# Dividing a block's weighted columns between ScalarE and VectorE in a graph network

## The chip, the cores and the metric

The kernel runs on one core of one Trainium2 chip. The core has TensorE (PE; its weight loads are listed as PEld), VectorE (DVE), ScalarE (ACT), GpSimd (POOL) and SyncE (SP), which run their own instruction streams in order and wait for one another by semaphores. The metric is the device time of one execution in microseconds. Three executions before the change took 3933.62, 3918.14 and 3926.89 us; the median is 3926.89 us.

## The reference

The input is a node table `x` of 6250 rows by 256 features, and 100,000 edges `src`, `dst`, sorted by `dst`. Two attention layers of one kind (four heads of 64 features, every node also an edge to itself), a residual with layer norm, then a third attention layer of another kind (eight heads of 32) and again a residual with layer norm. Cut to what matters:

```python
def _gatv2_layer(x, src, dst, n, Wl, Wr, att, b):          # H, C = 4, 64
    xl = (x @ Wl).reshape(n, H, C)
    xr = (x @ Wr).reshape(n, H, C)
    e = leaky_relu(xl[src] + xr[dst], 0.2)
    logits = einsum('ehc,hc->eh', e, att)
    alpha = exp(logits - segment_max(logits, dst)[dst]) / segment_sum(...)[dst]
    return segment_sum(xl[src] * alpha[:, :, None], dst).reshape(n, H * C) + b
...
h = _gatv2_layer(x, src, dst, n, Wl1, Wr1, att1, b1)        # layer one
h = elu(h)
h = _gatv2_layer(h, src, dst, n, Wl2, Wr2, att2, b2)        # layer two
x = _layernorm(x + h)
x = _layernorm(x + _L1_gnn_ref(x, W, a, src, dst))          # layer three
```

The change touches the product `xl[src] * alpha` of layers one and two.

## The kernel before

A first part (up to some 225 us of the profiled execution) builds tables of features in memory and orders the nodes by how many edges end in them. The nodes then form 49 blocks of 128, one node to a partition. In a block, each node's neighbours stand side by side as columns: a block with at most `c` edges to a node has `S = c + 1` columns, the first being the node itself. `S` is 39 in the first block, 26 in the second, 21 to 18 around the fifteenth, and 10 in the last; the 49 blocks have 863 columns, of which 814 are gathered. A column is 128 partitions by 4 heads by 64 features of fp32 (with one or two more numbers). The columns of a block are cut into chunks of at most nine (`chunks`), each in a buffer of its own; a pool of seven such buffers (`rowp`, `bufs=7`) lets gathers run ahead.

`layer2` runs layer one (i = 0) and layer two (i = 1) with the same loop over blocks `b`. Each engine takes its instructions in the order in which the loop writes them:

1. `start(b + 3)`, `gather(b + 1)`: POOL issues an indirect DMA for each column of the next block (L1311). In layer one `start` is one more indirect DMA on POOL (L1397), in layer two two loads on SP (L1439, L1440).
2. `ready(b + 1)`: the next block's own rows. In layer one PE transposes them (L1180), ScalarE copies the transpose (`xT`, L1182), PE multiplies (L1187); in layer two ScalarE copies a loaded row (L1446).
3. `attend(b)`: for each chunk VectorE takes the larger of gathered rows and own row (L1331), multiplies by the attention vector (L1332) and sums per head into the logits `lg` (L1333). Then `weights`: VectorE takes the largest logit (`top`, L1198), ScalarE makes four exponentials, one a head, into `wt` in PSUM with their sums `den` (L1205), and copies the weights of the last `few` columns to `by` in SBUF (L1212).
4. `end(b - 1)`: VectorE divides the sum of the block before, `acc`, by its `den` (`h`, L1348) and works on it further; ScalarE applies what is left (L1411 to L1414 in layer one, L1280 to L1288 in layer two).
5. VectorE takes the reciprocal of `den` (L1377).
6. `weighted_sum(b)`: the columns are multiplied by their weights in place. ScalarE takes the last `few` columns of the last chunk with one multiply for each column and head, 128 partitions by 64 features (L1234); VectorE takes all others with one multiply for each chunk (L1235). PE then adds up the columns in order by matmuls with an identity into `acc` in PSUM (L1242, two matmul records to a column, the second of which gives a signal).
7. The rest of block `b - 1`: PE transposes `h` or the normed row (L1180), ScalarE copies it (L1182), PE multiplies (L1187), ScalarE copies the result to a row (L1426 or L1461), SP stores it.

So a column that ScalarE weights is added on PE only after its four multiplies are signalled, and these columns are the last of the block. `few` is zero in the last block. The third layer has eight heads, passes no `few`, and adds up on VectorE.

Of the kernel before, what the change touches and what calls it, by code (L numbers as in the profile page):

```python
# [1120 lines left out]
def tile_by_degree(  # L1121
# [7 lines left out]
    NB = -(-N // P)  # L1129
# [12 lines left out]
    def per_head(t, H):  # L1142
        return t.rearrange("p (h d) -> p h d", h=H)
# [30 lines left out]
    def source(of, b, j):  # L1174
        return bass.IndirectOffsetOnAxis(ap=of[:, b, j : j + 1], axis=0)
# [13 lines left out]
    def chunks(n):  # L1189
        k = -(-n // T)  # L1190
        cut = [n * i // k for i in range(k + 1)]
        return list(zip(cut, cut[1:]))

    def weights(work, ps, lg, S, H, scalar=0):


        top = work.tile([P, H], F32, name="top")
        nc.vector.tensor_reduce(  # L1198
            top, lg[:, :S, :].rearrange("p s h -> p h s"), axis=AX.X, op=OP.max, negate=True
        )  # L1200
        wt = ps.tile([P, S, H], F32, name="wt")
        den = work.tile([P, H], F32, name="den")
        if H <= 4:
            for h in range(H):
                nc.scalar.activation(  # L1205
                    wt[:, :, h], lg[:, :S, h], AF.Exp, bias=top[:, h : h + 1],
                    accum_out=den[:, h : h + 1],
                )
            by = None
            if scalar:  # L1210
                by = work.tile([P, scalar, H], F32, name="by")
                nc.scalar.copy(by, wt[:, S - scalar :, :])  # L1212
            return (wt, by), lambda: den
        nc.vector.tensor_add(lg[:, :S, :], lg[:, :S, :], top[:, None, :].to_broadcast([P, S, H]))  # L1214
        nc.scalar.activation(wt, lg[:, :S, :], AF.Exp)  # L1215

        def add_up():
            nc.vector.reduce_sum(den, wt.rearrange("p s h -> p h s"), axis=AX.X)
            return den

        return (wt, None), add_up

    def weighted_sum(ps, rows, cut, wts, H, width, between):

        wt, by = wts
        acc = ps.tile([P, F], F32, name="acc")
        S = cut[-1][1]
        for g, (s0, s1) in zip(rows, cut):
            n = s1 - s0
            g4 = g[:, :n, : H * width].rearrange("p t (h d) -> p t h d", h=H)[:, :, :, : F // H]  # L1230
            m = n - by.shape[1] if by is not None and s1 == S else n
            for t in range(m, n):
                for h in range(H):
                    nc.scalar.mul(g4[:, t, h, :], g4[:, t, h, :], by[:, t - m, h : h + 1])  # L1234
            nc.vector.tensor_mul(  # L1235
                g4[:, :m], g4[:, :m],
                wt[:, s0 : s0 + m, :].unsqueeze(3).to_broadcast([P, m, H, F // H]),
            )
            if s0 == 0:
                between()  # L1240
            for t in range(n):
                nc.tensor.matmul(acc, ident, g4[:, t], start=s0 + t == 0, stop=s0 + t == S - 1)  # L1242
        return acc
# [46 lines left out]
    def layer2(i, table, of, width, start, own, finish):  # L1290
# [4 lines left out]
        with ExitStack() as es:  # L1295
            rowp = es.enter_context(tc.tile_pool(name=f"rows{i}", bufs=7))
            zp = es.enter_context(tc.tile_pool(name=f"z{i}", bufs=3))
            work = es.enter_context(tc.tile_pool(name=f"work{i}", bufs=3))
            ps = es.enter_context(tc.tile_pool(name=f"ps{i}", bufs=2, space=PSUM))
            ps1 = es.enter_context(tc.tile_pool(name=f"ps1{i}", bufs=1, space=PSUM))  # L1300
            pst = es.enter_context(tc.tile_pool(name=f"pst{i}", bufs=2, space=PSUM))
            at = ps1.tile([P, W2], F32, name="at")
            nc.scalar.copy(at, att[i])
            state = {}

            def gather(b):
                cut = chunks(cols[b] + 1)
                rows = [rowp.tile([P, T, width], F32, name="g") for _ in cut]
                for g, (s0, s1) in zip(rows, cut):
                    for s in range(max(s0, 1), s1):  # L1310
                        nc.gpsimd.indirect_dma_start(  # L1311
                            out=g[:, s - s0, :], out_offset=None, in_=table,
                            in_offset=source(of, b, s - 1),
                        )
                state[b] = [rows, cut]

            later = []

            def ready(b):
                pr, put = own(work, ps, pst, b, state[b][0][0][:, 0, :W2])  # L1320
                state[b].append(pr)
                later.append(put)

            def attend(b):
                rows, cut, xr = state.pop(b)
                S = cols[b] + 1
                lg = work.tile([P, CM + 1, H2], F32, name="lg")
                for g, (s0, s1) in zip(rows, cut):
                    n = s1 - s0
                    z = zp.tile([P, T, W2], F32, name="z")[:, :n, :]  # L1330
                    nc.vector.tensor_max(z, g[:, :n, :W2], xr[:, None, :].to_broadcast([P, n, W2]))  # L1331
                    nc.vector.tensor_mul(z, z, at[:, None, :].to_broadcast([P, n, W2]))  # L1332
                    nc.vector.reduce_sum(  # L1333
                        lg[:, s0:s1, :], z.rearrange("p t (h d) -> p t h d", h=H2), axis=AX.X
                    )
                few = min(S // 3, cut[-1][1] - cut[-1][0] - 1) if b + 1 < NB else 0
                wt, new = weights(work, ps, lg, S, H2, few)
                while later:
                    later.pop()()
                if i == 0:  # L1340
                    for g, (s0, s1) in zip(rows, cut):
                        s = max(s0, 1)
                        nc.scalar.copy(spots[:, b, s - 1 : s1 - 1], g[:, s - s0 : s1 - s0, W2])
                return rows, cut, wt, new

            def end(b, acc, den):
                h = work.tile([P, F], F32, name="h")
                nc.vector.tensor_mul(  # L1348
                    per_head(h, H2), per_head(acc, H2),
                    den.unsqueeze(2).to_broadcast([P, H2, D2]),  # L1350
                )
                if i == 0:
                    nc.vector.tensor_add(h, h, bias[0])
                return finish(work, pst, b, h)

            for b in range(3):
                start(work, b)
            gather(0)
            ready(0)
            later.pop()()  # L1360
            if i == 0:
                none(state[0][2])
            acc, den, rest = None, None, None
            for b in range(NB):
                if b + 3 < NB:
                    start(work, b + 3)
                if b + 1 < NB:
                    gather(b + 1)
                if b + 1 < NB:
                    ready(b + 1)  # L1370
                rows, cut, wt, new = attend(b)
                if b:
                    rest = end(b - 1, acc, den)
                if i == 0:
                    nc.vector.tensor_add(x1[:, b, :], x1[:, b, :], bias[1])
                den = new()
                nc.vector.reciprocal(den, den)  # L1377

                last = []

                def between():
                    if b:
                        last.append(rest())

                acc = weighted_sum(ps1, rows, cut, wt, H2, D2 + 1, between)
                if i == 0 and b + 1 < NB:
                    none(state[b + 1][2])
                if last:
                    last[0]()
            end(NB - 1, acc, den)()()  # L1390

    def none(t):

        nc.vector.memset(t.rearrange("p (h d) -> p h d", h=H2)[:, :, D2:], -BIG)
# [79 lines left out]
    with ExitStack() as es:  # L1474
# [59 lines left out]
        for b in range(NB):  # L1534
# [4 lines left out]
            rows, cut, wt, new = attend(b)  # L1539
# [41 lines left out]
```

## Time and profile before

| what | us |
|---|---|
| median of three executions | 3926.89 |
| the profiled execution | 3945.85 |
| its span, from the first to the last instruction | 3944.1 |
| first part and tables, up to | about 225 |
| layer one, from the first reciprocal at 225.3 to that of its last block at | 1452.4 |
| layer two, likewise, from 1534.5 to | 2689.5 |
| layer three and the end, up to | 3944.1 |
| VectorE busy over the span | 2724.0 (69%) |
| GpSimd busy | 2582.6 (65%) |
| TensorE matmuls busy | 1485.0 (38%) |
| ScalarE busy | 1102.9 (28%) |

Busy times are those of one profiled execution, which was 19 us over the median. GpSimd's busy time here is nearly all the issue of gathers. "issue" as the reason of an idle time means that the profile shows no instruction that ended it, "remote" that a signal ended it whose sender the profile doesn't tell. A group's line gives after the bar its busy time, the mean duration of one instruction in ns, and the idle time of the engine just before the group's instructions. In a timeline the columns are the start, the time taken, engine, line, operation, what is written and read, and the number of instructions merged; in brackets the idle time before and what ended it. A wait is recorded at the engine that waits; a signal's way from one engine to another is not.

### The profile page before, as it was taken

The page shows a single profiled execution, that of the slowest core. Times are in us where ns is not written, and L with a number is a line of the kernel's source. Part 1 is how long each engine was busy: PE and PEld are TensorE (multiplying, and loading weights), DVE is VectorE, ACT ScalarE, POOL GpSimd, SP SyncE. Part 2 cuts the span into 40 slices and gives each one's busy share as a digit, 9 for nine tenths or more (in the row PEclk, how much of TensorE's full clock was granted, in tenths as well). Part 3 has the DMA queues.
Part 4 walks back from the last instruction along what each step waited for, and adds up shares of the span by engine and source line. Part 5 has one row for each costly group of instructions (what it writes and reads, how often), then busy time and mean ns, then how long its engine had stood idle before and what let it go on. Part 6 is the DMA issues. An engine that isn't in the chain of part 4 may idle for free.

```text
span 3944.1 us, 23710 instructions
## 1 busy us (share of the span) xinstructions
PE 1485.0 (38%) x5144; PEld 1107.1 (28%) x5145; DVE 2724.0 (69%) x2731; ACT 1102.9 (28%) x4179; POOL 2582.6 (65%) x2640
## 2 busy tenths in 40 slices
PE   5336556556676761455545455552000000000000
PEld 4224434344554541343433343442000000000000
DVE  6277778678788876888877888983655545444554
ACT  2124334334444441343434343541000000000000
POOL 6466666666666636666666666654777777776675
PEclk7667778777788886777666767776555555555555
DMA  8443333333343424343333343433333333333332
GB/s 185 103 96 99 98 100 105 100 98 102 104 107 103 106 74 101 98 111 107 106 107 107 106 112 104 118 104 58 102 100 97 102 99 100 99 97 84 82 99 72
DMA packets 197564, 399.63 MB, mean 101 GB/s; under 512 B 63516, under 2 KB 115994, under 8 KB 197396
## 3 DMA queue, kind: packets, MB, share of 16 engines
q0 software_dynamic: 123488, 342.06, 33.6%
q1 hardware_dynamic: 66226, 54.22, 4.8%
q10 hardware_dynamic: 7698, 1.74, 0.4%
q8 instruction: 45, 0.74, 0.1%
q14 instruction: 107, 0.88, 0.1%
HBM read 357.84 MB, written 40.42 MB: 101 GB/s over the span
## 4 chain that ended last, share of the span: by engine, by line
issue 23%; POOL 22%; DVE 15%; PE 13%; another core or an unknown queue 9%; ACT 6%; DMA 2%; DVEq 0%; ACTq 0%; POOLq 0%
POOL g L1485 15%; PE acc L1242 9%; POOL g L1311 5%; DVE z L1332 4%; DVE z L1331 4%; PE pm L1187 3%; ACT g L1234 3%; DVE lg L1333 2%; ACT wt L1205 2%; DVE g L1235 1%; DVE g L1253 1%; POOL out L1525 1%; ACT xT L1182 1%; DMA g<-whs_d,spots 1%
## 5 line engine op out<-in xcount | busy, mean ns | idle before, releaser
L1242 PE MATMUL acc<-g,ident 128*128 128x256 f32 x3452 | 1038.7, 462 | 940.8 <-issue 368.9
L1242 PEld LDWEIGHTS acc<-g,ident 128*128 128x128 f32 x3452 | 778.1, 233 | 1197.6 <-issue 618.4
L1311 POOL DMA_INDIRECT g<-xl_d,spots x814 | 772.5, 949 | 465.2 <-issue 227.5
L1311 POOL DMA_INDIRECT g<-xl_d,near_r x814 | 774.8, 952 | 427.8 <-issue 239.2
L1485 POOL DMA_INDIRECT g<-whs_d,spots x814 | 857.3, 1053 | 299.0 <-issue 292.6
L1234 ACT ACTIVATE g<-g,by 128x64 f32<-128x64 f32 x2064 | 560.2, 337 | 431.4 <-issue 429.4
L1331 DVE TENSOR_TENSOR z<-g,pr 128x1820 f32<-128x1820 f32 (+4 forms) x236 | 502.3, 2129 | 60.9 <-DMA g<-xl_d,spots 31.9
L1332 DVE TENSOR_TENSOR z<-z,at 128x1820 f32<-128x1820 f32 (+4 forms) x236 | 503.8, 2135 | 8.1
L1333 DVE TENSOR_REDUCE lg<-z 128x28 f32<-128x1820 f32 (+4 forms) x236 | 503.6, 2134 | 8.2
L1235 DVE TENSOR_TENSOR g<-g,wt 128x1792 f32<-128x1792 f32 (+5 forms) x236 | 354.0, 1518 | 2.9
L1215 ACT ACTIVATE wt<-lg 128x128 f32<-128x128 f32 (+17 forms) x49 | 14.0, 285 | 849.3 <-DVE lg L1214 245.2
L1496 DVE TENSOR_TENSOR lg<-g,s_r 128x56 f32<-128x56 f32 (+4 forms) x113 | 25.1, 223 | 314.3 <-DMA g<-whs_d,spots 281.8
L1253 DVE TENSOR_TENSOR g<-g,wt 128x1792 f32<-128x1792 f32 (+4 forms) x113 | 229.5, 2049 | 0.0
L1182 ACT COPY xT<-pt 128x256 f32<-128x256 f32 x147 | 55.0, 374 | 581.9 <-PE pt L1180 341.8
L1377 DVE RECIPROCAL den<-den 128x4 f32<-128x4 f32 x98 | 17.4, 178 | 240.6 <-ACT wt L1205 186.3
L1205 ACT ACTIVATE wt<-lg,top 128x19 f32<-128x19 f32 (+14 forms) x392 | 116.1, 296 | 219.9 <-DVE lg L1333 129.1
L1348 DVE TENSOR_TENSOR h<-acc,den 128x256 f32<-128x256 f32 x98 | 40.9, 417 | 158.6 <-remote 91.6
L1187 PE MATMUL pm<-wcat,xT 128*128 128x260 f32 x392 | 136.2, 506 | 35.9 <-ACT xT L1182 34.5
L1262 DVE TENSOR_TENSOR g<-g,g 128x1792 f32<-128x1792 f32 (+4 forms) x64 | 129.1, 2017 | 25.2 <-DVE g L1253 15.7
L1187 PE MATMUL pm<-wh_cat,xT 128*128 128x272 f32 x196 | 83.2, 564 | 128.9 <-ACT xT L1182 80.3
L1187 PEld LDWEIGHTS pm<-wcat,xT 128*128 128x128 f32 x392 | 95.5, 257 | 71.5 <-ACT xT L1182 50.9
L1525 POOL DMA_INDIRECT out<-y,node_i x49 | 51.4, 1049 | 70.0 <-ACT y L1288 54.4
(162 smaller groups left out, 1575.5 us busy)
## 6 DMA issues: line engine op xcount, KB each, us to landing
g<-xl_d,near_r POOLq DMA_INDIRECT x814
g<-xl_d,spots POOLq DMA_INDIRECT x814
g<-whs_d,spots POOLq DMA_INDIRECT x814
whs_d<-row SPq DMA_DIRECT2D x49, 132.0 KB
xl_d<-xl SPq DMA_DIRECT2D x49, 130.0 KB
xl_d<-row SPq DMA_DIRECT2D x49, 130.0 KB
xr_d<-row SPq DMA_DIRECT2D x49, 130.0 KB
two<-xl_d SPq DMA_DIRECT2D x49, 130.0 KB
```

Source lines behind the costliest of these rows:

```text
L1187: nc.tensor.matmul(pm, xT[:, c, :], w[:, c, :], start=c == 0, stop=c == 1)
L1205: nc.scalar.activation(wt[:, :, h], lg[:, :S, h], AF.Exp, bias=top[:, h : h + 1], accum_out=den[:, h : h + 1],)
L1234: nc.scalar.mul(g4[:, t, h, :], g4[:, t, h, :], by[:, t - m, h : h + 1])
L1235: nc.vector.tensor_mul(g4[:, :m], g4[:, :m], wt[:, s0 : s0 + m, :].unsqueeze(3).to_broadcast([P, m, H, F // H]),)
L1242: nc.tensor.matmul(acc, ident, g4[:, t], start=s0 + t == 0, stop=s0 + t == S - 1)
L1253: nc.vector.tensor_mul(g4, g4, wt[:, s0:s1, :].unsqueeze(3).to_broadcast([P, n, H, width]))
L1262: nc.vector.tensor_add(t[:, :m], t[:, :m], u[:, :m])
L1311: nc.gpsimd.indirect_dma_start(out=g[:, s - s0, :], out_offset=None, in_=table, in_offset=source(of, b, s - 1),)
L1331: nc.vector.tensor_max(z, g[:, :n, :W2], xr[:, None, :].to_broadcast([P, n, W2]))
L1332: nc.vector.tensor_mul(z, z, at[:, None, :].to_broadcast([P, n, W2]))
L1333: nc.vector.reduce_sum(lg[:, s0:s1, :], z.rearrange("p t (h d) -> p t h d", h=H2), axis=AX.X)
L1485: nc.gpsimd.indirect_dma_start(out=g[:, s - s0, :], out_offset=None, in_=wh_d[:, :], in_offset=source(spots, b, s),)
```

## The change

In `attend` of `layer2`, `few` was a third of the block's columns and is now a sixth, both rounded down and kept below the size of the last chunk. VectorE's multiply of the last chunk takes the columns that ScalarE gives up.

```diff
-                few = min(S // 3, cut[-1][1] - cut[-1][0] - 1) if b + 1 < NB else 0
+                few = min(S // 6, cut[-1][1] - cut[-1][0] - 1) if b + 1 < NB else 0
                 wt, new = weights(work, ps, lg, S, H2, few)
```

`weights` copies the weights of `few` columns to `by`; `weighted_sum` reads their number from the shape of `by`:

```python
m = n - by.shape[1] if by is not None and s1 == S else n
for t in range(m, n):
    for h in range(H):
        nc.scalar.mul(g4[:, t, h, :], g4[:, t, h, :], by[:, t - m, h : h + 1])
nc.vector.tensor_mul(
    g4[:, :m], g4[:, :m],
    wt[:, s0 : s0 + m, :].unsqueeze(3).to_broadcast([P, m, H, F // H]),
)
```

A block of 18 to 23 columns goes from 6 or 7 columns on ScalarE to 3, one of 15 to 17 from 5 to 2, one of 12 to 14 from 4 to 2. Over the 48 blocks that have any, ScalarE's columns go from 258 to 122 in each of the two layers.

## The prediction

> **What bounds the kernel now.** I read the page first, then busy time by stage, then the waits of VectorE in each stage, then the timeline of neighbouring blocks. Layer one runs from 225 to 1452 us, layer two from 1534 to 2690 us; the rest doesn't execute the changed lines. Columns: stretch, then PE, PEld, DVE, ACT and POOL busy.
>
> ```profile
> 225.00:1452.00 1227.00, 772.35 (x2646) 566.68 (x2646) 982.53 (x837) 521.32 (x1958) 771.17 (x810) 0.79 0.38 100
> 1534.00:2690.00 1156.00, 602.94 (x1988) 454.70 (x1988) 973.57 (x792) 460.16 (x1845) 724.88 (x764) 0.72 0.39 104
> ```
>
> VectorE is the busiest, at 80% and 84%; ScalarE is at 40%. The question is what VectorE waits for in the other fifth. The groups of VectorE, for 300 to 1430 us and then 1600 to 2660 us, put it before two lines (after the bar: busy us, mean ns, idle us before the group, and what ended it):
>
> ```profile
> L1348 DVE TENSOR_TENSOR h<-acc,den 128x256 f32<-128x256 f32 x45 | 18.8, 417 | 63.6 <-PE acc L1242 33.9 <-remote 19.9 <-PE pt L1180 9.7
> ...
> L1377 DVE RECIPROCAL den<-den 128x4 f32<-128x4 f32 x45 | 8.0, 178 | 155.5 <-ACT wt L1205 114.6 <-issue 40.9
> ```
>
> ```profile
> L1348 DVE TENSOR_TENSOR h<-acc,den 128x256 f32<-128x256 f32 x45 | 18.7, 416 | 59.2 <-remote 46.9 <-PE acc L1242 10.4 <-PE pt L1180 1.9
> ...
> L1377 DVE RECIPROCAL den<-den 128x4 f32<-128x4 f32 x44 | 7.8, 178 | 78.3 <-ACT wt L1205 67.3 <-issue 10.9
> ```
>
> So VectorE waits for the sum over neighbours (acc, from PE) and for the softmax weights of the next block (wt, from ScalarE). Why are these late? Two neighbouring blocks of 19 columns, 24 ScalarE multiplies (six columns by four heads) each, differ. In the first, ScalarE's timeline:
>
> ```profile
> 681.76 2.41 ACT L1234 ACTIVATE g<-g,by 128x64 f32<-128x64 f32 x9
> ...
> 703.65 0.35 ACT L1234 ACTIVATE g<-g,by 128x64 f32<-128x64 f32 x1 [1.08 <-issue]
> ```
>
> Nine multiplies run back to back, the other fifteen come about 1.4 us apart, until 704.0. PE takes a ScalarE column only when its four multiplies are signalled: columns two, three and four at 692.41, 698.04 and 702.27 us, and the last two in
>
> ```profile
> 703.73 2.07 PE L1242 MATMUL acc<-g,ident 128*128 128x256 f32 x4 [0.24 <-remote]
> ```
>
> VectorE had finished that iteration's logits at 701.6 and sat idle twice:
>
> ```profile
> 705.84 0.42 DVE L1348 TENSOR_TENSOR h<-acc,den 128x256 f32<-128x256 f32 x1 [4.23 <-PE acc L1242]
> ...
> 713.03 0.18 DVE L1377 RECIPROCAL den<-den 128x4 f32<-128x4 f32 x1 [5.97 <-issue]
> ```
>
> The second idle time is the same lateness: on PE the transposes of h stand behind the sum, and on ScalarE the copies xT and row (706.27 to 710.93), then xT again, stand ahead of the exponentials, which start at 711.22. That block took 33.1 us from reciprocal to reciprocal. The next one ran its ScalarE multiplies thus:
>
> ```profile
> 714.86 2.48 ACT L1234 ACTIVATE g<-g,by 128x64 f32<-128x64 f32 x10
> ...
> 723.05 2.50 ACT L1234 ACTIVATE g<-g,by 128x64 f32<-128x64 f32 x10 [1.07 <-issue]
> ```
>
> Slow again, until POOL stopped issuing gathers, for want of a buffer, from 720.55 to
>
> ```profile
> 723.93 0.95 POOL L1311 DMA_INDIRECT g<-xl_d,near_r  x1 [3.38 <-ACT g L1234]
> ```
>
> and 2.5 us into that pause the last ten went at once. VectorE's idle time there is the floor:
>
> ```profile
> 736.52 0.18 DVE L1377 RECIPROCAL den<-den 128x4 f32<-128x4 f32 x1 [0.71 <-ACT wt L1205]
> ```
>
> That block took 23.5 us. I conclude: while gathers are being issued, completion signals from ScalarE and PE get through at about one per 0.7 us (ScalarE's steps are 0.7 or 1.4 us), and a multiply costs a signal, not its 337 ns. In layer two the records show it less openly:
>
> ```profile
> 2017.47 5.83 ACT L1234 ACTIVATE g<-g,by 128x64 f32<-128x64 f32 x24
> 2044.18 0.37 ACT L1182 COPY xT<-pt 128x256 f32<-128x256 f32 x1 [20.89 <-remote]
> ```
>
> All 24 are over by 2023.3, yet PE's last pair for that block starts at 2031.13 and VectorE gets acc at 2044.14.
>
> **What the Trainium skill says.** "Perfetto Trace Analysis", section DVE / Act Engine Instruction, ends a record when the update is pushed; its propagation comes after, unrecorded. The trace agrees: 2023.3 against 2031.13 above. "TensorE: Matmul & The Clock Gate", section The cost: per-tile semaphore tail, says increments serialize, at 26.3 ns each; here the steps are 0.7 to 1.4 us, so the measurement decides. "SBUF — State Buffer", section Who interferes with whom, gives ScalarE ports of its own; nothing in the trace contradicts it, so I don't blame SBUF for the slow multiplies.
>
> **The change part by part.** From the code, the columns left to ScalarE fall per layer from 258 to 122: 136 move, in 48 of 49 blocks (three per block in 31 of them). The instruction order on every engine stays; the same VectorE multiplies get longer and runs of ScalarE multiplies shorter. No DMA or wait is added.
>
> Removed: 2 x 136 x 4 = 1088 of the 2064 multiplies, 1088 x 337 ns = 367 us of ScalarE busy time, worth nothing in itself as ScalarE is at 40%. Its worth is in the lateness. Added to VectorE, the bound: two forms of L1235,
>
> ```profile
> L1234 ACT ACTIVATE g<-g,by 128x64 f32<-128x64 f32 x2064 | 560.2, 337 | 431.4 <-issue 429.4 <-DMA g<-xl_d,spots 1.1
> ...
> L1235 DVE TENSOR_TENSOR g<-g,wt 128x1536 f32<-128x1536 f32 x34 | 59.5, 1753 | 0.8
> ...
> L1235 DVE TENSOR_TENSOR g<-g,wt 128x768 f32<-128x768 f32 x46 | 43.6, 948 | 0.0
> ```
>
> differ by three columns and 805 ns, 268 ns a column. ("VectorE: DVE Perf Modes", Why PSUM operands drop a tier, has fp32 with a PSUM operand at one element a cycle; at the 0.96 GHz of its Specifications 256 elements are 267 ns.) 272 x 268 ns = 73 us, all on the path: nothing hides it.
>
> What can go: the idle time above the floor. Layer one 63.6 + 155.5 - 45 x 0.71 = 187 us; layer two 59.2 + 78.3 - 44 x 0.4 (the undisturbed idle in its timeline) = 120 us; 307 together. How much goes? In the first block above, twelve multiplies instead of 24 would have given PE its last ScalarE column at 698.04 rather than about 703.7, 5.7 us of the 9.5 us that this block is longer than its neighbour: 60%. Blocks of 15 to 17 columns keep eight multiplies, signalled by 692.41 on the same clock, 11 us earlier, more than the 3 to 4 us that they wait. Against that, PE's own signals, one a column, stay. I take two thirds, 205 us; the bounds are nothing and all 307. Late next is VectorE itself: its idle time falls to the floor.
>
> Sum: -205 + 73 = -132 us. The profiled execution took 3945.85 us (span 3944.1), so its like would be 3814; the median shown is 19 us lower, 3926.89, and gives 3795.
>
> **Rivals.**
> - PE's own signals (slower). Each column gives one whatever engine weighted it, 1726 over both layers. If these fill the slow path, PE's sum is as late as before; the layer-two block speaks for it, 12 us between PE's last pair and acc. Against: in the first block PE's signal was at VectorE by 705.84, on its last matmul. With one sixth of the idle time gone: -51 + 73, 3949; with none, 4000. It decides once less than 73/307, 24%, goes. Chance 0.10.
> - POOL becomes the bound: 814 gathers a layer at 1.255 us from start to start, and 49 more loads in layer one, are 1083 and 1022 us of 1227 and 1155. VectorE's floor after the change is 1227 - 187 + 36 = 1076 in layer one, so both engines are nearly even, POOL seldom pauses, and signals stay slow in part. For it: pauses freed the signals above. Against: seven buffers let it run ahead. With 44% gone: -135 + 73, 3865. Chance 0.22.
> - Everything goes: -307 + 73, 3693. For it: the last two blocks of layer one, with no gathers in flight, ran their twelve multiplies in 2.96 us without a gap. Chance 0.10.
>
> That the change does less than it says isn't open: the smaller counts stand in the program.
>
> **How the numbers follow.** Two thirds, between half (3846) and 85% (3739), has 0.58 and is the forecast. The range 3705 to 3900 reaches into POOL's case and most of the way to everything; it leaves out the slow rival. This measurement tells a change from none at about 0.5%, 20 us. Slower, 0.08, and no change, 0.05, come from the first rival and the edge of the second; faster has 0.87.
>
> **What would show it.** Right: L1234 x976, its idle "issue" of 429.4 us mostly gone; L1235 busy up by 73 us; the idle time before L1348 and L1377 in both layers down to some 100 us above the floor; the third layer's length unchanged. Wrong: idle before L1348 still ended by "remote" with PE long done (PE's signals), or VectorE waiting before L1331 for gathers (POOL).

## The result, and the profile after

| ten executions each | median us | range |
|---|---|---|
| before | 3921.74 | 3912.89 to 3933.62 |
| after | 3932.30 | 3919.63 to 3952.38 |

The ratio is 1.003, with a 95% interval of 1.0013 to 1.0048: no gain, and a loss of 5 to 19 us. The profiled execution took 3952.38 us (span 3950.6), 6.5 us over that of before. The kernel before took 3922 us in this comparison and 3936 us in one later series (a series is a set of executions taken together), but 3524 to 3533 us in nine others: in the first two the profiles show signals between engines arriving late, in the others at once, so I call them late and prompt series and compare the time of each kernel only with that of the kernel before in its own series.

VectorE's two waits over the whole execution, before:

```profile
L1377 DVE RECIPROCAL den<-den 128x4 f32<-128x4 f32 x98 | 17.4, 178 | 240.6 <-ACT wt L1205 186.3
...
L1348 DVE TENSOR_TENSOR h<-acc,den 128x256 f32<-128x256 f32 x98 | 40.9, 417 | 158.6 <-remote 91.6
```

And the groups on the page of after:

```profile
L1235 DVE TENSOR_TENSOR g<-g,wt 128x1792 f32<-128x1792 f32 (+6 forms) x236 | 426.4, 1824 | 2.0
...
L1182 ACT COPY xT<-pt 128x256 f32<-128x256 f32 x147 | 54.9, 373 | 1067.2 <-remote 670.3
...
L1234 ACT ACTIVATE g<-g,by 128x64 f32<-128x64 f32 x976 | 251.0, 335 | 65.4 <-issue 65.1
...
L1377 DVE RECIPROCAL den<-den 128x4 f32<-128x4 f32 x98 | 17.4, 177 | 189.5 <-ACT wt L1205 157.3
...
L1348 DVE TENSOR_TENSOR h<-acc,den 128x256 f32<-128x256 f32 x98 | 40.7, 415 | 138.3 <-remote 127.1
```

ScalarE's multiplies are fewer and stutter much less: 65.1 us of "issue" instead of 429.4. VectorE's multiply (L1235) has grown from 354.0 to 426.4 us, +72.4. But its idle time before L1348 and L1377, 158.6 + 240.6 = 399.2 us before, is still 138.3 + 189.5 = 327.8 us: 71 us went, 72 us came. Stage by stage, VectorE's waits for 300 to 1430 us and then for 1600 to 2660 us:

```profile
L1348 DVE TENSOR_TENSOR h<-acc,den 128x256 f32<-128x256 f32 x44 | 18.3, 415 | 58.8 <-remote 58.8
...
L1377 DVE RECIPROCAL den<-den 128x4 f32<-128x4 f32 x44 | 7.8, 178 | 133.7 <-ACT wt L1205 109.7 <-issue 24.0
```

```profile
L1348 DVE TENSOR_TENSOR h<-acc,den 128x256 f32<-128x256 f32 x45 | 18.7, 415 | 68.3 <-remote 68.3
...
L1377 DVE RECIPROCAL den<-den 128x4 f32<-128x4 f32 x45 | 8.0, 177 | 48.5 <-ACT wt L1205 41.1 <-issue 7.4
```

Before L1348 all of it is now "remote", a signal whose sender isn't told, where in layer one of the kernel before PE's sum ended over half of it. What that means is seen in one block of 19 columns, the same in both kernels. First its timeline before:

```profile
738.35 2.01 ACT L1234 ACTIVATE g<-g,by 128x64 f32<-128x64 f32 x8
...
760.17 1.22 PE L1242 MATMUL acc<-g,ident 128*128 128x256 f32 x2 [4.37 <-remote]
...
761.55 0.35 ACT L1234 ACTIVATE g<-g,by 128x64 f32<-128x64 f32 x1 [1.08 <-issue]
...
765.13 1.22 PE L1242 MATMUL acc<-g,ident 128*128 128x256 f32 x2 [3.74 <-remote]
...
769.33 1.22 PE L1242 MATMUL acc<-g,ident 128*128 128x256 f32 x2 [2.98 <-remote]
...
770.09 0.94 POOL L1311 DMA_INDIRECT g<-xl_d,near_r  x1 [6.24 <-remote]
...
770.58 0.42 DVE L1348 TENSOR_TENSOR h<-acc,den 128x256 f32<-128x256 f32 x1 [12.42 <-PE acc L1242]
...
777.81 0.18 DVE L1377 RECIPROCAL den<-den 128x4 f32<-128x4 f32 x1 [6.01 <-ACT wt L1205]
```

And after:

```profile
737.24 2.46 ACT L1234 ACTIVATE g<-g,by 128x64 f32<-128x64 f32 x9
...
742.90 0.35 ACT L1234 ACTIVATE g<-g,by 128x64 f32<-128x64 f32 x1 [1.06 <-issue]
...
752.76 1.22 PE L1242 MATMUL acc<-g,ident 128*128 128x256 f32 x2 [4.89 <-remote]
...
753.77 0.63 PE L1180 MATMUL pt<-ident,h 128*128 128x128 f32 x2
...
768.49 0.42 DVE L1348 TENSOR_TENSOR h<-acc,den 128x256 f32<-128x256 f32 x1 [10.64 <-remote]
768.53 0.37 ACT L1182 COPY xT<-pt 128x256 f32<-128x256 f32 x1 [25.28 <-remote]
768.90 0.94 POOL L1311 DMA_INDIRECT g<-xl_d,near_r  x1 [5.98 <-ACT xT L1182]
...
774.78 0.18 DVE L1377 RECIPROCAL den<-den 128x4 f32<-128x4 f32 x1 [5.08 <-ACT wt L1205]
```

The multiplies end at 743.25 instead of 761.9, PE's last column at 754.0 instead of 770.55, and the transposes that follow it at 754.4. Yet VectorE gets the sum, and ScalarE the transposes, only at 768.5, 14 us later. That is 33.4 us into the block, against 34.1 us in the kernel before, where ScalarE's late multiplies seemed to be the reason. What both have in common is a pause of POOL: it had no free buffer, had issued nothing for 6.24 us before and 5.98 us after, and the waits end as that pause ends.

The trace also records when semaphores are updated, which the views above don't print. Before, updates of ScalarE's semaphore are recorded at 760.13, 765.08 and 769.28 us, and PE's last three columns start at 760.17, 765.13 and 769.33, 0.04 to 0.05 us after each. So here PE takes a column every 4 to 5 us, as ScalarE's signals come in, and the last comes 7 us after the last multiply. After, PE's own updates are the late ones: two, at 761.13 and 766.03, and then ten from 768.12 to 768.50, 42 ns apart, though PE's work was over at 754.4. POOL's last issue had ended at 762.92.

To see how much of the idle time is of this kind, I took each of the 96 blocks with a successor in layers one and two, from reciprocal to reciprocal, and subtracted the durations of VectorE's instructions from its length. Blocks that lose over 8 us against the others (none lies between 6.9 and 8.6 us):

```text
                        multiplies  blocks over 8 us   the other blocks
after                       976       13: 228 us            91 us
before                     2064       15: 208 us           173 us
```

In the kernel before, 14 of the 15 long ones have L1348 start within 1.3 us of the end of a POOL pause of over 1.5 us, against 8 of the 81 others; after, 8 of 13 within 0.5 us, and in three of the other five the second wait ends within such a pause. So most long stalls end with a pause of POOL. That the pause ends the stall isn't shown: POOL waits for signals too (for ScalarE's, or for a "remote" one, at the end of the two pauses above), so a signal that is late enough makes both, and no run separates the two readings. The change halved the short stalls and left the long ones.

### The profile page after: what moved, and what is told of

It is laid out like the page before. It is cut to its first block, busy times and chain, and to the rows that moved or that the text cites. A ratio compares the mean times of both kernels' runs of the same rounds, so it can differ in the third digit from the quotient of the medians.

```text
span 3950.6 us, 22419 instructions
## 1 busy us (share of the span) xinstructions
PE 1406.7 (36%) x5145; PEld 1098.2 (28%) x5145; DVE 2794.7 (71%) x2731; ACT 799.7 (20%) x3091; POOL 2579.9 (65%) x2640
## 3 DMA queue, kind: packets, MB, share of 16 engines
q0 software_dynamic: 123488, 342.06, 33.4%
q1 hardware_dynamic: 66226, 54.22, 4.8%
## 4 chain that ended last, share of the span: by engine, by line
DVE 22%; issue 22%; POOL 18%; another core or an unknown queue 14%; PE 8%; ACT 7%; DMA 2%; DVEq 0%; ACTq 0%; POOLq 0%
POOL g L1485 15%; DVE z L1332 6%; DVE z L1331 6%; PE acc L1242 5%; DVE lg L1333 3%; PE pm L1187 3%; DVE g L1235 3%; ACT wt L1205 3%; POOL g L1311 2%; ACT g L1234 2%; DVE g L1253 1%; POOL out L1525 1%; DMA g<-xl_d,spots 1%; DMA g<-whs_d,spots 1%
## 5 line engine op out<-in xcount | busy, mean ns | idle before, releaser
L1242 PE MATMUL acc<-g,ident 128*128 128x256 f32 x3452 | 949.8, 441 | 776.0 <-issue 367.2
L1242 PEld LDWEIGHTS acc<-g,ident 128*128 128x128 f32 x3452 | 765.4, 225 | 966.1 <-issue 697.8
L1331 DVE TENSOR_TENSOR z<-g,pr 128x1820 f32<-128x1820 f32 (+4 forms) x236 | 502.1, 2128 | 59.6 <-DMA g<-xl_d,spots 31.6
L1235 DVE TENSOR_TENSOR g<-g,wt 128x1792 f32<-128x1792 f32 (+6 forms) x236 | 426.4, 1824 | 2.0
L1234 ACT ACTIVATE g<-g,by 128x64 f32<-128x64 f32 x976 | 251.0, 335 | 65.4 <-issue 65.1
L1187 PE MATMUL pm<-wcat,xT 128*128 128x260 f32 x392 | 149.5, 547 | 204.6 <-ACT xT L1182 181.6
L1377 DVE RECIPROCAL den<-den 128x4 f32<-128x4 f32 x98 | 17.4, 177 | 189.5 <-ACT wt L1205 157.3
L1348 DVE TENSOR_TENSOR h<-acc,den 128x256 f32<-128x256 f32 x98 | 40.7, 415 | 138.3 <-remote 127.1
L1187 PE MATMUL pm<-wh_cat,xT 128*128 128x272 f32 x196 | 74.3, 513 | 172.1 <-issue 101.2
```

Of the source, the lines that this page charges most:

```text
L1187: nc.tensor.matmul(pm, xT[:, c, :], w[:, c, :], start=c == 0, stop=c == 1)
L1235: nc.vector.tensor_mul(g4[:, :m], g4[:, :m], wt[:, s0 : s0 + m, :].unsqueeze(3).to_broadcast([P, m, H, F // H]),)
```

## Experiments

**Without ScalarE's columns.** Label f0: `few` is nothing, so VectorE weights all columns.

```diff
-                few = min(S // 6, cut[-1][1] - cut[-1][0] - 1) if b + 1 < NB else 0
+                few = 0
```

> The changed kernel with no column for ScalarE (few = 0): VectorE takes the 244 columns that ScalarE still had, at 268 ns each +65 us. Theory A (a ScalarE multiply costs a signal, as in the prediction): taking away the last 976 multiplies takes away most of what is left of VectorE's idle time before L1348 and L1377 (328 us in the changed kernel, some 65 us of it a floor), so 3932 - 200 + 65 = about 3800. Theory B (PE's signals, one a column whatever engine weighted it, make the lateness): the idle time stays within 50 us of 328, so 3932 + 65 = about 4000, ratio to before 1.02.

3638.48 us against 3530.9, ratio 1.0308 (1.0291 to 1.0325). Neither theory had this: the kernel before itself took 391 us less than in the first comparison, and VectorE hardly waits (its groups in this kernel):

```profile
L1348 DVE TENSOR_TENSOR h<-acc,den 128x256 f32<-128x256 f32 x98 | 40.6, 415 | 11.0 <-PE acc L1242 11.0
...
L1377 DVE RECIPROCAL den<-den 128x4 f32<-128x4 f32 x98 | 17.4, 178 | 54.2 <-ACT wt L1205 54.2
```

**Plain loads for the gathers.** Labels a_sp (changed kernel) and b_sp (before). SP loads 128 consecutive rows for each column, which aren't the neighbours of the graph:

```diff
-                        nc.gpsimd.indirect_dma_start(
-                            out=g[:, s - s0, :], out_offset=None, in_=table,
-                            in_offset=source(of, b, s - 1),
-                        )
+                        r = (b + s) % NB * P
+                        nc.sync.dma_start(g[:, s - s0, :], table[r : r + P, :])
```

> The changed kernel, but in layers one and two every gathered column is a plain load of 128 consecutive table rows issued by SP instead of an indirect gather issued by POOL, so the neighbours weighted and summed aren't those of the graph; bytes, buffers and all instructions on PE, ScalarE and VectorE are the same. Theory C (signals are slow because POOL is issuing gathers): PE's signals arrive at once, VectorE's idle time before L1348 and L1377 falls from 328 to under 100 us, and ScalarE's issue idle before L1234 (65 us) goes: 3932 - 230 = about 3700 or less. Theory D (the lateness comes from the DMA traffic or from the engines' own order, not from POOL's issuing): the idle time stays near 328 and the time near 3930.

> The kernel before with the same replacement of the gathers by plain loads on SP (neighbours not those of the graph). Theory C: without slow signals VectorE is at its floor in both kernels and the third on ScalarE is simply the better division: 73 us less than a_sp, about 3625, with ScalarE's issue idle before L1234 (429 us before) gone. Theory D: 3920, and no better than a_sp by more than 20 us.

Same series: 3556.25 us, ratio 1.0071 (1.0054 to 1.0088), and 3485.14 us, ratio 0.987 (0.9853 to 0.9886). With VectorE hardly waiting for gathered rows (14.9 us before L1329, which is L1331 here, in both) the two divisions differ by 71 us, the added 72 us nearly in full. As to theory C they tell nothing here, as f0 has prompt signals with POOL's gathers in flight.

**Two columns to a matmul.** Labels a_pair (changed kernel) and b_pair (before); the odd column of a chunk keeps a matmul of its own.

```diff
-        acc = ps.tile([P, F], F32, name="acc")
+        acc = ps.tile([P, 2, F], F32, name="acc")
...
-                nc.tensor.matmul(acc, ident, g4[:, t], start=s0 + t == 0, stop=s0 + t == S - 1)
+                    nc.tensor.matmul(acc, ident, g4[:, t : t + 2], start=s0 + t == 0, stop=s0 + t == S - 2)
...
+                nc.vector.reduce_sum(h, acc.rearrange("p a f -> p f a"), axis=AX.X)
                 nc.vector.tensor_mul(
-                    per_head(h, H2), per_head(acc, H2),
+                    per_head(h, H2), per_head(h, H2),
```

> The changed kernel, in which PE adds two columns with one matmul (512 wide, into two halves of acc), so PE gives about 900 signals instead of 1726; VectorE adds the two halves in one more reduction before L1348, estimated at 512 x 1.05 ns = 0.54 us, 98 times, +53 us. Theory B (PE's signals): the lateness, 328 - 65 = 263 us of idle, halves: 3932 - 130 + 53 = about 3855. Theory A (the multiplies' signals): the lateness stays, 3932 + 53 = about 3985.

3594.32 us, ratio 1.0181 (1.0164 to 1.0198), in the same prompt series: no test of B. Nor are 53 us lost, as far as the changed kernel's 1.0162 in the next series tells. VectorE's groups say why:

```profile
L1352 DVE TENSOR_REDUCE h<-acc 128x256 f32<-128x512 f32 x98 | 66.7, 681 | 10.1 <-PE acc L1246 10.1
...
L1382 DVE RECIPROCAL den<-den 128x4 f32<-128x4 f32 x98 | 15.9, 162 | 3.7 <-ACT wt L1205 3.6
```

The reduction stands where VectorE waited 0.55 us a block for ScalarE's exponentials; that wait, 54.2 us in f0, is down to 3.7, and the reduction takes its place.

**Both kernels again.** Labels after_again and before_again, no edit.

> The changed kernel itself, unaltered. In the four runs so far the kernel before took 3531 us instead of 3922, and three kernels with POOL's gathers or without them had no idle time above the floor. Theory E (slow signals are a condition of the chip or of the run, which the program doesn't set; where it is absent VectorE is at its floor in both kernels, so only the added work shows): idle before L1348 and L1377 under 80 us, and the time is that of before plus 73 us, 3604 if before is 3531 again, ratio 1.021. If the chip has slow signals again (before near 3922): ratio 1.003 as on record. Theory F (before and after have slow signals wherever they run, and the four kernels escaped them each by its edit): ratio 1.003 at either level of before.

> The kernel before itself, for its profile beside the run above. Theory E: if it takes 3531, ScalarE's issue idle before L1234 is under 10 us instead of 429, and VectorE's idle time before L1348 and L1377 under 80 us instead of 399; if it takes 3922, both are as on record. Theory F: 429 and 399 at either level.

On another chip: 3588.62 us, ratio 1.0162 (1.0145 to 1.0179); before against itself 0.9994 (0.9978 to 1.0009). Theory E. Groups of the kernel before (its ScalarE multiplies, from the page: 502.0 us busy, 0.0 idle), then of the changed one:

```profile
L1331 DVE TENSOR_TENSOR z<-g,pr 128x1820 f32<-128x1820 f32 (+4 forms) x236 | 502.5, 2129 | 65.7 <-DMA g<-xl_d,spots 29.1 <-DMA g<-xl_d,near_r 22.5 <-DMA near_r<-near_d,node_i 12.3
...
L1235 DVE TENSOR_TENSOR g<-g,wt 128x1792 f32<-128x1792 f32 (+5 forms) x236 | 354.1, 1518 | 2.9
...
L1348 DVE TENSOR_TENSOR h<-acc,den 128x256 f32<-128x256 f32 x98 | 40.6, 414 | 10.4 <-PE acc L1242 10.4
...
L1377 DVE RECIPROCAL den<-den 128x4 f32<-128x4 f32 x98 | 17.4, 178 | 54.1 <-ACT wt L1205 54.1
```

```profile
L1331 DVE TENSOR_TENSOR z<-g,pr 128x1820 f32<-128x1820 f32 (+4 forms) x236 | 502.3, 2128 | 53.1 <-DMA g<-xl_d,spots 29.1 <-DMA g<-xl_d,near_r 16.1 <-DMA near_r<-near_d,node_i 6.2
...
L1235 DVE TENSOR_TENSOR g<-g,wt 128x1792 f32<-128x1792 f32 (+6 forms) x236 | 426.6, 1825 | 2.0
...
L1348 DVE TENSOR_TENSOR h<-acc,den 128x256 f32<-128x256 f32 x98 | 40.6, 414 | 9.7 <-PE acc L1242 9.7
...
L1377 DVE RECIPROCAL den<-den 128x4 f32<-128x4 f32 x98 | 17.4, 178 | 54.3 <-ACT wt L1205 54.3
```

Where signals are prompt the idle time that the prediction wanted to remove isn't there: 64.5 us and 64.0 us. What the change adds is paid, 72.5 us, but for 12.6 us that VectorE waits less for gathers before L1331 as it asks for them later; the profiled spans differ by 57.7 us. The block of 19 columns ahead of the one that stalled above (the prediction's second block), in the timeline of the kernel before with prompt signals:

```profile
606.05 5.82 ACT L1234 ACTIVATE g<-g,by 128x64 f32<-128x64 f32 x24
...
617.27 0.37 ACT L1182 COPY xT<-pt 128x256 f32<-128x256 f32 x1 [5.40 <-PE pt L1180]
...
625.77 0.41 DVE L1348 TENSOR_TENSOR h<-acc,den 128x256 f32<-128x256 f32 x1
...
627.70 0.18 DVE L1377 RECIPROCAL den<-den 128x4 f32<-128x4 f32 x1 [0.72 <-ACT wt L1205]
```

All 24 multiplies run in 5.82 us without a gap, and PE's sum lies ready before VectorE wants it.

**Half of the columns.** Label f2: `S // 2` in place of `S // 6`, still kept below the last chunk; 2568 multiplies.

> ScalarE takes half of a block's columns instead of a third, as before kept below the size of the last chunk: blocks of 10 to 18 columns go from 3 to 6 columns on ScalarE to 4 to 8, blocks of 19 or more hardly change. By the sizes of the chunks that is some 130 columns more over both layers, 130 x 268 ns = 35 us off VectorE against the kernel before. If signals are prompt again (before near 3531): ScalarE at 18 us of a block's 22 us still keeps up, POOL's gathers become late in the small blocks and give back a third (as they gave 14 of the 72 us when the columns went the other way): 3531 - 22 = 3509, ratio 0.994. If signals are slow (before near 3922): theory A (a multiply costs a signal) has it slower than before, 3922 + 50 or more; theory B (PE's signals alone) has it faster, 3922 - 30.

Prompt again: 3501.07 us, ratio 0.9936 (0.9919 to 0.9952), as expected. It is better than the kernel before there, by 23 us, and shows which way the division should have gone where signals are prompt.

**More DMA completions.** Label b_load, on the kernel before:

```diff
+            extra = es.enter_context(tc.tile_pool(name=f"extra{i}", bufs=8))
...
                             in_offset=source(of, b, s - 1),
                         )
+                        for _ in range(2):
+                            nc.sync.dma_start(extra.tile([P, 8], F32, name="more"), x[:P, :8])
```

> The kernel before, in which every gather of layers one and two is followed by two small plain loads on SP (128 rows of 32 bytes each into a scratch tile that nobody reads), so about three times as many DMA completions are signalled while gathers are in flight. Theory G (signals get slow when the program's own DMA completions fill the path that they share): ScalarE's issue idle before L1234 and VectorE's idle time before L1348 and L1377, 0 and 64 us with prompt signals, come back to hundreds of us and the time goes from 3525 or 3531 towards 3900. Theory H (the program's own signals aren't what made them slow; the condition comes from outside the program): both idle times stay within 30 us of what they were, and the time within 1.5%, up to 3580, for the loads' own share of the DMA engines.

3535.78 us, ratio 1.0019 (1.0003 to 1.0035). The trace records 95,223 DMA completions instead of the 46,737 of the kernel before with prompt signals; in layers one and two alone 73,737 instead of 28,881, 2.6 times as many. The page's queue of plain DMAs and ScalarE's multiplies:

```profile
q1 hardware_dynamic: 535090, 67.77, 12.8%
...
L1234 ACT ACTIVATE g<-g,by 128x64 f32<-128x64 f32 x2064 | 501.9, 334 | 0.0
```

Eight times the packets on that queue (66,226 in the kernel before) and 2.6 times the completions don't make signals late. That speaks against G up to this load; that the condition comes from outside the program (H) rests on the same program having been late and prompt.

**A full half, over chunk borders.** Label f2u, on the changed kernel: `few = S // 2`, 3312 multiplies (the 4128 in what was expected is a slip); VectorE is busy for 2637.6 us instead of 2724.0 before.

```diff
-            m = n - by.shape[1] if by is not None and s1 == S else n
+            first = S - (by.shape[1] if by is not None else 0)
+            m = min(max(first - s0, 0), n)
...
-                few = min(S // 6, cut[-1][1] - cut[-1][0] - 1) if b + 1 < NB else 0
+                few = S // 2 if b + 1 < NB else 0
```

> ScalarE takes a full half of a block's columns, over chunk borders where need be: 414 columns a layer instead of 258 (before) or 321 (half, kept below the last chunk). VectorE loses 2 x 156 x 268 ns = 84 us against the kernel before. With prompt signals: if VectorE alone were the bound, 3525 - 84 = 3441. If POOL's gathers are next (814 a layer at some 1.2 us, 977 us of layers that take about 1004 to 1043 in the kernel before), the idle time before L1331 grows by what is gained beyond that: layer one 1043 - 42 = 1001 against 977 + 49 loads x 1.2 us = 1036 of POOL, so about half of it is given back and the time is some 3485 (ratio 0.989), hardly under the 3501 of the half kept below the last chunk. If signals are slow (before near 3922): 4128 - 2064 x 0.2 or more multiplies only add signals, slower than before.

This run fell on a late series: 3986.33 us against 3935.83, ratio 1.0115 (1.0091 to 1.0139). ScalarE stutters (445.9 us of issue idle), and VectorE, with less to do, waits more for the exponentials, 302.0 us instead of 240.6, and less for the sum, 100.5 us instead of 158.6 (L1235, L1348 and L1377 of the other kernels are L1239, L1352 and L1381 here, and ScalarE's multiply is L1235):

```profile
L1235 ACT ACTIVATE g<-g,by 128x64 f32<-128x64 f32 x3312 | 865.2, 336 | 450.8 <-issue 445.9
...
L1381 DVE RECIPROCAL den<-den 128x4 f32<-128x4 f32 x98 | 17.4, 178 | 302.0 <-ACT wt L1205 232.7
```

By blocks, as above: 15 lose over 8 us, 257 us together, the others 264 us. With before and after that makes a line: short stalls of 91, 173 and 264 us for 976, 2064 and 3312 multiplies, (173 - 91)/1088 = 0.075 and (264 - 173)/1248 = 0.073 us a multiply. It can't go on to no multiplies, where it would leave 18 us; the same sum is 47 us in the prompt profile of the kernel before. The long ones, 228, 208 and 257 us, follow no such line, but in f2u they aren't plainly of one kind with the others: their border is arbitrary there (7.1, 7.6, 8.0 and 10.2 us are neighbours), L1352 starts near the end of a POOL pause in 2 of 15, and the second wait ends within such a pause in 7 more. At these sizes f2u's loss is 91 us of short and 49 us of long stalls more than before against 86 us less work for VectorE.

**Attempts at another late series.** Labels f0_c, b_pair and b_sp_c in one, b_pair_d and b_sp_d, f0_e and b_sp_e, b_sp_f, and f2_sp (half of the columns with plain loads), to ask there which signals are late and whether POOL's gathers are needed for it.

> No column for ScalarE, again, for a chip with slow signals (the first comparison and the last run had before at 3922 and 3936; the chips of the other runs at 3524 to 3532). If before is near 3930 this time: theory A (a multiply costs a signal) has most of the 328 us of idle time before L1348 and L1377 of the changed kernel gone and pays 65 us for 244 columns: 3932 - 200 + 65 = about 3800, ratio 0.97. Theory B (PE's signals, one a column, make the lateness): idle near 328, 3932 + 65 = about 4000, ratio 1.018. If the idle time only goes on falling as from before to after (71 us for 1088 multiplies, so 64 for the last 976): 3932 - 64 + 65, ratio 1.003. If before is near 3530: 1.031, as measured.

> The kernel before with two columns to a PE matmul, so half of PE's signals, and the reduction that adds the two halves (681 ns, 98 times, 67 us[...]). If before is near 3930: theory B has half of the lateness gone, 399 - 65 = 334, half of it 167: 3930 - 167 + 55 = about 3820, ratio 0.97. Theory A: nothing of it goes, 3930 + 55 = 3985, ratio 1.014. If before is near 3530: 3530 + 55 less some 12 that POOL gives back, ratio 1.012.

> The kernel before with plain loads on SP for the gathers of layers one and two (neighbours not those of the graph), again for a chip with slow signals. If before is near 3930: theory C (signals are slow there only while POOL has indirect gathers in flight) gives 3485 plus some 60 us for layer three and the tables, which keep POOL's gathers: about 3550, ratio 0.90, and no issue idle before L1234. Theory D (the chip's signals are slow beside any DMA traffic of this volume): within 2% of before, 3860 to 3990, with some 400 us of issue idle before L1234. If before is near 3530: 0.987, as measured.

> The kernel before with two columns to a PE matmul. On a chip with prompt signals 1.003, as measured (3537). On one with slow signals (before near 3930): theory B (PE's signals make the lateness) has about half of 334 us of idle time above the floor gone and pays what the added reduction costs on a prompt chip, 8 us to 55 us: 3930 - 167 + 30 = about 3795, ratio 0.966. Theory A (ScalarE's multiplies make it, PE's signals don't matter): 3930 + 30 = 3960, ratio 1.008.

> The kernel before with plain loads on SP for the gathers of layers one and two (neighbours not those of the graph). On a chip with prompt signals 0.987, as measured (3485). On one with slow signals: theory C (slow only while POOL has indirect gathers in flight) 3485 + 60 for layer three and the tables, 3550, ratio 0.90, and ScalarE's issue idle before L1234 gone. Theory D (slow beside any DMA traffic of this volume): within 2% of before, with some 400 us of issue idle before L1234.

> No column for ScalarE. On a chip with prompt signals 1.031, as measured (3638). On one with slow signals (before near 3930): by the slope of the runs there, 71 us of idle time for 1088 multiplies, the last 976 take 64 us with them and cost 65: ratio 1.003, as the changed kernel has. Theory A as predicted (what is left of the lateness is the multiplies'): 0.97. Theory B (all that is left is PE's signals'): 1.018.

> The kernel before with plain loads on SP for the gathers of layers one and two (neighbours not those of the graph). On a chip with prompt signals 0.987, as measured twice. On one with slow signals: theory C (slow only while POOL has indirect gathers in flight) 3550, ratio 0.90, and ScalarE's issue idle before L1234 gone. Theory D (slow beside any DMA traffic of this volume): within 2% of before, with some 400 us of issue idle before L1234.

> The kernel before with plain loads on SP for the gathers of layers one and two (neighbours not those of the graph). On a chip with prompt signals 0.987. On one with slow signals: theory C (slow only while POOL has indirect gathers in flight) 3550, ratio 0.90. Theory D (slow beside any DMA traffic of this volume): within 2% of before, with some 400 us of issue idle before L1234.

> ScalarE with half of the columns, kept below the last chunk, and plain loads on SP for the gathers of layers one and two (neighbours not those of the graph). With prompt signals: 126 columns x 268 ns = 34 us under the same with a third (3485), 3451, ratio 0.978, if POOL's gathers gave back the rest in the kernel with gathers (23 us of 34 measured); 3462, ratio 0.981, if something else did. On a chip with slow signals: theory C (slow only while POOL has indirect gathers in flight) about 3515, ratio 0.895; theory D (slow beside any DMA traffic of this volume) 3880 to 4000.

All were prompt, so their question stays open. What they repeat: f0 1.031 (1.0292 to 1.0327) and 1.0303 (1.0286 to 1.032); b_sp 0.9876, 0.9863, 0.9868 and 0.9882. New is b_pair, 1.0027 (1.0016 to 1.0038) and 1.0018 (1.0011 to 1.0025): with half of PE's signals the time isn't shorter where signals are prompt, and the 67 us of reduction cost 6 to 8 us, not 55: the multiply after it (L1353) takes 426 ns where L1348 took 414, and what hides most of the reduction is the wait before the reciprocal, 3.7 us instead of 54.1. f2_sp took 3457.18 us, ratio 0.9803 (0.9787 to 0.982), between the two values expected, so how much POOL gives back with half of the columns isn't settled by it. They also tell that lateness isn't a chip's fixed trait: f2u's late series and the prompt one of b_pair_d ran on a chip of the same number, some seventeen minutes apart.

## Why the prediction was wrong

- **VectorE is the bound, and a column costs it 268 ns.** Right: 272 columns, +72.4 us measured for 73 expected, in the late and in the prompt series, and nothing hides it but 12.6 us of waiting for gathers where signals are prompt.
- **ScalarE's stutter.** Right as far as it goes: L1234 x976, its "issue" idle down by 364 us. The third layer takes what it took, 1254.5 us from the end of layer two before and 1252.4 after.
- **"How much goes? ... I take two thirds, 205 us."** This is the step that failed: of the idle time before the two lines 71 us went, 21% of the 335 that lie above the 64.5 us of a prompt series (in the prediction's own stretches 47 of its 307 us, 15%). It rested on one block of 33.1 us in which the last multiply set the end, and on the belief that "a multiply costs a signal" wherever the time is lost. In the sum it is 205/1088 = 0.19 us a multiply, where 71/1088 = 0.065 us were measured; by blocks the short stalls show 0.075 us and the long ones no fall. Over half of the lost time, 208 of 381 us, is in 15 long stalls, of which 14 end near the end of a pause of POOL. The block shown above, two on from the one that I worked from, has it: its multiplies end 17 us earlier in the block, and VectorE is served 0.7 us earlier, because PE's signals are then the late ones. Nor do signals come at "about one per 0.7 us" there: ScalarE's are recorded 4 to 5 us apart, PE's ten together at the end.
- **The cost of a column on ScalarE in a late series** is then 4 x 0.075 = 0.30 us of short stalls, against 0.268 us of VectorE. The two prices are nearly the same, which fits a change that moves so little; the 9 us that they would leave as a gain are outweighed by 20 us more of long stalls. This is worked out from three profiles of single executions, and the first price comes in part from the very difference that it is to explain.
- **The rival with PE's signals** came nearest: it decides "once less than 73/307, 24%, goes", and 15 to 21% went; its 3949 us with one sixth gone stand beside 3932. Its mark in the profile is there as well: "idle before L1348 still ended by 'remote' with PE long done", 127.1 of 138.3 us. That PE's signals come late is shown in the block above, matmuls over at 754.4 us and their readers starting at 768.5 us; that it is their number that makes them late, so that fewer would have helped, wasn't shown, as both kernels with half of them met prompt signals.
- **POOL as the bound** didn't come about: its idle time before the gathers of layers one and two is 907.6 us after and 893.0 us before, it pauses for over 1.5 us 97 times there instead of 96, and VectorE waits 59.6 us before L1331 instead of 60.9. In the prompt profile of the kernel before there are 8 such pauses, 27 us together instead of 375. So the pauses come with the late signals; whether they also let the signals through, as the prediction has it, stays open.
- **Unasked:** whether the idle time belonged to the program. The kernel before is some 400 us faster in nine of eleven series, without any edit, and every profile of such a series has the idle time gone. There the change, as far as measured, is a plain loss of 1.6%.

Open is what makes signals late, why ScalarE's multiplies stutter, as the profile names nothing that they wait for, whether the lateness needs POOL's gathers, and whether half of PE's signals would shorten the long stalls. None of the runs that would tell fell on a late series.

## What to carry to other kernels

Split idle time by stalls and by what ends each before pricing its removal, and take more than one block: here removing instructions ahead of the waits shortened the short stalls and left the long ones, which end in another way. Run an unchanged kernel on more than one occasion before tuning away a wait; an idle time of 335 us (399.2 - 64.5) here came and went with the occasion, and the edit made against it costs 1.6% when it is absent. Work for the bound engine is nearly free where it falls into a wait that it has anyway: in a prompt series a reduction of 67 us put ahead of the exponentials' wait cost 6 to 8 us.

## What the hardware showed that I hadn't expected

The same program, with the same 342.06 MB gathered, took 3922 and 3936 us in two series and 3524 to 3533 us in nine. Parts that the change doesn't touch are longer too: in the profiles of the kernel before, the first part takes 225.3 us late and 201.3 prompt, layer three with the end 1254.5 and 1197.1. The transfers don't take longer: the packets of POOL's queue took 33.6% of 3944.1 us, 1325 us, and 37.9% of 3528.4 us, 1337 us. Nor do instructions: a gather's issue takes 949 and 952 ns in the two layers when late and 946 and 949 ns when prompt. What differs is how semaphore updates are recorded as arriving, in the profiles of the kernel before:

```text
recorded updates       late (3944.1 us)   prompt (3528.4 us)
DMA completions              8,465             46,737
PE's semaphore               1,868              2,292
ScalarE's semaphore          1,368              2,606
VectorE's semaphore          1,490              2,689
```

In the late profile a DMA of POOL leaves 2.2 to 2.6 records of its completion on average, in the prompt one 16.0. The program gives 2290, 2606 and 2687 updates of the three engines' semaphores, so in the prompt profile practically every one is recorded. Whether in the late one several updates arrive together or only their records are missing, the counts alone don't tell; that PE starts 0.05 us after a recorded update of ScalarE's, in the block above, speaks for the former. In the last two blocks of layer one, where no gathers are in flight, VectorE loses 0.6 us a block in the late profile as in the prompt one; but so little is lost in other late blocks too, 34 of 96 lose under 1 us, so this doesn't show that the lateness needs gathers.
